# Preparing the weights of a folded CIN network: T with V2 stationary on four tiles of TensorE, turned two fields at a time, on one Trainium2 core

## The chip, the cores and the metric

The kernel runs on one core of one Trainium2 chip. The metric is the device time of one execution in microseconds, taken as the median of several runs: 757.2 us before the change (three runs, 756.5 to 758.38). The profile was taken from a run of its own, whose span from the first to the last instruction is 755.9 us. All data are fp32.

## The reference

A compressed interaction network of three layers, on a batch of 1024 samples with 39 fields of 64 elements:

```python
def _cin_layer(Xk, X0, W, b):                 # Xk (B, Hk, E), X0 (B, 39, E), W (64, Hk*39)
    Wr = W.reshape(64, Hk, 39)
    return einsum('bhe,bfe,ohf->boe', Xk, X0, Wr) + b[None, :, None]

Xk = X0
for W, b in ((W0, b0), (W1, b1), (W2, b2)):   # W0 (64, 39*39), W1 and W2 (64, 64*39)
    Xk = _cin_layer(Xk, X0, W, b)
    outs.append(Xk.sum(axis=-1))
y = concatenate(outs, -1) @ fc_w.T + fc_b     # fc_w (1, 192), y (1024, 1)
```

Only a linear function of the last two layers is wanted. So the kernel folds them: V2[o, b] is W2 contracted with the last third of fc_w, with the second third of fc_w as a 40th column, and T[h, a, b] is the sum over o of W1[o, h, a] times V2[o, b]. Then both the first layer X1[h] and its factor are quadratic forms in the fields (the factor with linear terms, for which a row of ones stands as field 40):

- X1[h] = sum over (a, b) of W0[h, a, b] x_a x_b
- Z[h] = sum over (a, b) of T[h, a, b] x_a x_b
- the result is, up to bias terms, the sum over h and the 64 elements of X1[h] times (Z[h] + fc_w[h])

## The kernel before

It has two stages. **Preparation** loads the weights, makes V2, then T and W0 with h on the partitions, in one tile `both` of 128 partitions (W0 on 0 to 63, T on 64 to 127) by 39 x 40 columns (a, b), and from that the stationary matrices: x_a x_b and x_b x_a are the same product, so their weights are added, in seven chunks of up to 128 pairs; each chunk is turned on TensorE and copied to `wa`. **The main stage** goes through 32 blocks of 2048 columns (32 samples of 64 elements); VectorE (DVE) multiplies gathered rows of fields into a tile `p` of 128 pair products, and TensorE multiplies `wa` by it.

Sizes and the tiles of the preparation:

```python
B, F, E, H = 1024, 39, 64, 64
FH = F * H
NPAIR = 6; ORDER = (0, 1, 3, 2, 4, 5); NCHUNK = NPAIR + 1
MM, SUB, BLK = 512, 1024, 2048
NA = 20; NG0 = 6; FT = F + 1
...
v2 = const.tile([H, FT], F32, name="v2")
both = const.tile([128, F * FT], F32, name="both")
...
w1s = prep.tile([H, FH], F32, name="w1s")
w0s = prep.tile([2 * F, NA * H], F32, name="w0s")
...
load(0)                                                                 # x for the first block, on SyncE's queue
nc.scalar.dma_start(fcrow, fc_w)
nc.scalar.dma_start(w2s, w2.rearrange("o (s n) -> (o s) n", s=2))
load_ones(0, nc.scalar)
nc.sync.dma_start(w1s, w1)                                              # L201
nc.scalar.dma_start(                                                    # L202
    w0s, bass.AP(w0t.tensor, w0t.offset, [[F * H, F], [(F - NA) * H, 2], [1, NA * H]])
)
```

W0 comes as (b, a, h). TensorE is kept occupied by multiplications of zeros (`spin`); V2 comes from eight matmuls on four tiles of 32 columns (L305), a transpose on DVE and copies:

```python
def spin(n):
    for _ in range(n):
        nc.tensor.matmul(idle[:, 0:128], zeros[:, 0:128], zeros[:, 0:128], start=True, stop=True)   # L224
spin(4)
...
for k in range(2):
    for u in range(4):
        f0 = u // 2 * 19 + k * 10
        nc.tensor.matmul(pv[k][32 * u : 32 * u + 32, 0:320], fc2[:, u % 2 * 32 : u % 2 * 32 + 32],  # L305
                         w2v[:, f0 : f0 + 10, :], start=True, stop=True)
...
spin(5)
for k in range(2):
    nc.vector.transpose(blocks[:, k], pv[k][:, 0:320])
```

T takes one matmul for each field a, with W1's columns of that field stationary and V2's 40 columns moving; W0 takes one transpose for two fields; both land in the four banks `pt`, which are copied to `both`:

```python
w1v = w1s.rearrange("o (h f) -> o f h", f=F)

def turn_t(g):
    for a in range(g * NG0, min((g + 1) * NG0, NA)):
        for s in range(2):
            at = (s * NG0 + a % NG0) * FT
            nc.tensor.matmul(pt[g][H:128, at : at + FT], w1v[:, a + s * (F - NA), :], v2,           # L358
                             start=True, stop=True)

turn_t(0)
for a in range(NA):
    at = a % NG0 * FT
    nc.tensor.transpose(halves_of[a // NG0][0:H, at : at + F, :],                                   # L369
                        w0s[:, a * H : a * H + H], unit[0 : 2 * F, 0 : 2 * F])
for g in range(1, 4):
    turn_t(g)
first = [prods.tile([128, BLK], F32, name="p", tag="p") for _ in range(3)]
for g in range(4):
    n = min(NG0, NA - g * NG0)
    if g % 2 == 0:
        k = g // 2
        product(0, ORDER[k], halves[0], first[k])                                                   # L165
    for s in range(2):
        ...
        (nc.vector.tensor_copy, nc.scalar.copy)[g % 2](                                             # L387
            both[:, a * FT : (a + n) * FT], pt[g][:, at : at + n * FT])
spin(4)
```

The start of the main stage. `weight_rows(c)` makes the additions of chunk c (L402 on DVE, a few plain copies on ScalarE), `weight_turn(c)` turns it (L437) and copies it to `wa` (L438), `product` makes p (L165), and `multiply` is the multiplication of the main stage (L453) for quarters of 512 columns:

```python
for c in ORDER[:3]:
    weight_rows(c)
weight_turn(0)
p = {(0, c): t for c, t in zip(ORDER, first)}
product(0, ORDER[2], halves[0], first[2])
for n, c in steps[:3]:
    product(n, c, halves[1], p[n, c])
n, c = steps[3]
weight_rows(c)
p[n, c] = product(n, c)
for k, (n, c) in enumerate(steps[:3]):
    multiply(n, c, p[n, c], (0,))
    if k < 2:
        weight_turn(steps[k + 1][1])
    multiply(n, c, p[n, c], (1,))
```

The rows that `product` multiplies come by indirect transfers (L124) into `rt`, four tiles of 128 x 2048 a block, double buffered; products are made four steps ahead of their multiplication, in four buffers.

Of the kernel before, what the change touches and what calls it, by code (L numbers as in the profile page):

```python
# [54 lines left out]
F32 = mybir.dt.float32  # L55
# [22 lines left out]
NA = 20  # L78
NG0 = 6
# [18 lines left out]
def cin_kernel(ctx: ExitStack, tc: tile.TileContext, x, w0t, b0, w1, b1, w2, b2, fc_w, fc_b, out):  # L98
# [43 lines left out]
    v2 = const.tile([H, FT], F32, name="v2")  # L142
# [28 lines left out]
    with prep as prep:  # L171
        w2s = prep.tile([128, FH // 2], F32, name="w2s")
        w1s = prep.tile([H, FH], F32, name="w1s")
        w0s = prep.tile([2 * F, NA * H], F32, name="w0s")
# [13 lines left out]

        nc.vector.memset(ones, 1.0)
        nc.vector.memset(zeros, 0.0)  # L190
        nc.vector.memset(fc2, 0.0)
        nc.vector.memset(warm, 0.0)

        def load_ones(k, engine):
# [6 lines left out]
        nc.sync.dma_start(w1s, w1)  # L201
        nc.scalar.dma_start(  # L202
            w0s, bass.AP(w0t.tensor, w0t.offset, [[F * H, F], [(F - NA) * H, 2], [1, NA * H]])
        )
# [5 lines left out]
        nc.gpsimd.memset(pairs, 0.0)  # L210
        nc.scalar.copy(warm, warm)
# [6 lines left out]
        idle = bank("idle")  # L218
        pt = [bank("pt") for _ in range(4)]


        def spin(n):
            for _ in range(n):
                nc.tensor.matmul(idle[:, 0:128], zeros[:, 0:128], zeros[:, 0:128], start=True, stop=True)  # L224

        spin(4)


# [61 lines left out]
        spin(3)  # L290
# [21 lines left out]
        for k in range(3):  # L312
            turn_row(small[0:H, k + 1 : k + 2], k)
        turn_row(small[H:128, 4:5], 0)

        for g in range(4):
            nc.tensor.matmul(
                pt[g][0:H, F : 2 * NG0 * FT : FT],
                zeros[:, 0:H],
                zeros[:, 0 : 2 * NG0],  # L320
                start=True,
                stop=True,
            )
        spin(5)
# [3 lines left out]
        nc.scalar.copy(v2[:, F:FT], small[0:H, 2:3])  # L328
        nc.vector.tensor_copy(v2[:, 0:20], column[0:H])
        nc.scalar.copy(v2[:, 20:F], column[H:128, 1:20])  # L330
# [19 lines left out]

        w1v = w1s.rearrange("o (h f) -> o f h", f=F)
        halves_of = [t[:, 0 : 2 * NG0 * FT].rearrange("p (s c) -> p c s", s=2) for t in pt]

        def turn_t(g):
            for a in range(g * NG0, min((g + 1) * NG0, NA)):
                for s in range(2):
                    at = (s * NG0 + a % NG0) * FT
                    nc.tensor.matmul(  # L358
                        pt[g][H:128, at : at + FT],
                        w1v[:, a + s * (F - NA), :],  # L360
                        v2,
                        start=True,
                        stop=True,
                    )

        turn_t(0)
        for a in range(NA):
            at = a % NG0 * FT
            nc.tensor.transpose(  # L369
                halves_of[a // NG0][0:H, at : at + F, :],  # L370
                w0s[:, a * H : a * H + H],
                unit[0 : 2 * F, 0 : 2 * F],
            )
        for g in range(1, 4):
            turn_t(g)

        first = [prods.tile([128, BLK], F32, name="p", tag="p") for _ in range(3)]
        bothv = both.rearrange("p (a b) -> p a b", b=FT)
        for g in range(4):
            n = min(NG0, NA - g * NG0)  # L380
            if g % 2 == 0:
                k = g // 2
                product(0, ORDER[k], halves[0], first[k])
            for s in range(2):
                a = g * NG0 + s * (F - NA)
                at = s * NG0 * FT
                (nc.vector.tensor_copy, nc.scalar.copy)[g % 2](  # L387
                    both[:, a * FT : (a + n) * FT], pt[g][:, at : at + n * FT]
                )
        spin(4)  # L390


    def weight_rows(c):
# [233 lines left out]
```

## Time and profile before

| what | from the profile before |
|---|---|
| time, median of three runs | 757.2 us |
| span of the profiled run | 755.9 us |
| L453, main multiplication | 1792 records, first start 27.03 us |
| L358, matmuls of T | 80 records, 11.77 to 14.84 and 17.58 to 24.45 us |
| L369, transposes of W0 | 20 records, 14.84 to 17.58 us |
| L305, V2 | 16 records, from 5.83 us, 2.56 us busy |
| L387, copies to `both` | 4 of 128x240 on DVE (400 ns each), 2 of 128x240 and 2 of 128x80 on ScalarE |
| L402, additions | 50 in all, 22 of them from 24.88 us within 2.28 us |
| share of the DMA engines, 12 to 22 us | 0.97 to 1.04 |

In the profile PE is TensorE's matmul, PEld its weight load, DVE is VectorE, ACT is ScalarE and POOL is GpSimd. A line of a group has the line of the kernel, the engine, the operation, the tiles (output, then inputs), the shapes and the count; then busy time and mean length of one; then the idle time just before it and what ended it. An fp32 matmul leaves two records, a transpose one. Records of matmuls overlap, so the number of a group times its mean is more than its busy time. The page's second part divides the span into 40 slices and gives each engine's busy share in tenths, and under PEclk the clock granted to TensorE.

### The profile page before, as it was taken

The page shows a single profiled execution, that of the slowest core. Times are in us where ns is not written, and L with a number is a line of the kernel's source. Part 1 is how long each engine was busy: PE and PEld are TensorE (multiplying, and loading weights), DVE is VectorE, ACT ScalarE, POOL GpSimd, SP SyncE. Part 2 cuts the span into 40 slices and gives each one's busy share as a digit, 9 for nine tenths or more (in the row PEclk, how much of TensorE's full clock was granted, in tenths as well). Part 3 has the DMA queues.
Part 4 walks back from the last instruction along what each step waited for, and adds up shares of the span by engine and source line. Part 5 has one row for each costly group of instructions (what it writes and reads, how often), then busy time and mean ns, then how long its engine had stood idle before and what let it go on. Part 6 is the DMA issues. An engine that isn't in the chain of part 4 may idle for free.

```text
span 755.9 us, 5394 instructions
## 1 busy us (share of the span) xinstructions
PE 749.7 (99%) x1977; PEld 335.9 (44%) x1977; DVE 641.6 (85%) x504; ACT 161.3 (21%) x218; POOL 312.9 (41%) x192
## 2 busy tenths in 40 slices
PE   8999999999999999999999999999999999999998
PEld 6644444444444444444444444444444444444443
DVE  4688988888898888898888988888889888898885
ACT  1132122111122212122221112212122221212212
POOL 5765432635324362432536333363442536343100
PEclk8699999999999999999999999999999999999999
DMA  8889577665768657577765758766576864737400
GB/s 269 338 303 362 171 319 256 244 264 186 281 205 334 243 194 293 170 279 257 285 253 179 282 183 331 255 228 272 170 271 239 317 239 164 289 138 298 167 0 0
DMA packets 58698, 180.08 MB, mean 238 GB/s; under 512 B 37050, under 2 KB 37147, under 8 KB 38512
## 3 DMA queue, kind: packets, MB, share of 16 engines
q0 software_dynamic: 24160, 169.39, 59.1%
q1 hardware_dynamic: 34225, 9.30, 5.4%
q10 hardware_dynamic: 287, 1.06, 0.5%
q8 instruction: 15, 0.25, 0.1%
q14 instruction: 11, 0.09, 0.0%
HBM read 179.67 MB, written 10.28 MB: 251 GB/s over the span
## 4 chain that ended last, share of the span: by engine, by line
PE 98%; DMA 1%; DVE 0%; SPq 0%; ACT 0%; issue 0%
PE po L453 96%; PE pt L358 1%; DMA w1s<-in_w 1%; PE pt L369 0%; PE idle L224 0%; SPq L117 0%; PE tr L437 0%; DVE g L492 0%; DVE sums L494 0%; ACT zq L491 0%; ACT wa L438 0%; DVE y L582 0%; PE py L578 0%; PE pk L500 0%; PE pk L501 0%
## 5 line engine op out<-in xcount | busy, mean ns | idle before, releaser
L453 PE MATMUL po<-p,wa 128*128 128x512 f32 (+1 forms) x1792 | 723.5, 596 | 0.4 <-ACT wa L438 0.4
L165 DVE TENSOR_TENSOR p<-r 128x2048 f32<-128x2048 f32 (+1 forms) x195 | 435.0, 2258 | 93.6 <-PE po L453 87.8
L453 PEld LDWEIGHTS po<-p,wa 128*128 128x128 f32 (+1 forms) x1792 | 313.9, 190 | 406.2 <-issue 384.8
L124 POOL DMA_INDIRECT r<-xd,lists x131 | 258.8, 1975 | 374.6 <-DVE p L165 336.7
L472 ACT ACTIVATE z<-po,fc0s 64x512 f32<-64x512 f32 x124 | 84.6, 683 | 356.6 <-PE po L453 349.8
L466 ACT COPY g<-u 39x1024 f32<-39x1024 f32 x64 | 66.6, 1043 | 180.0 <-DVE sums L483 180.0
L478 DVE SCALAR_TENSOR_TENSOR g<-po,b0s,z 64x512 f32<-64x512 f32 x124 | 86.4, 734 | 0.0
L483 DVE TENSOR_REDUCE sums<-g 103x16 f32<-103x1024 f32 x62 | 75.6, 1220 | 2.2
L167 DVE TENSOR_TENSOR p<-u,v 128x2048 f32<-128x2048 f32 x16 | 36.6, 2285 | 0.0
L124 POOL DMA_INDIRECT u<-xd,lists x16 | 28.4, 1773 | 10.2 <-DMA xd<-in_x 5.7
L124 POOL DMA_INDIRECT v<-xd,lists x16 | 16.2, 1010 | 4.9 <-issue 4.9
L358 PE MATMUL pt<-v,w1s 64*64 64x40 f32 x80 | 10.0, 311 | 1.1 <-DMA w1s<-in_w 1.1
L358 PEld LDWEIGHTS pt<-v,w1s 64*64 64x64 f32 x80 | 9.8, 212 | 1.4 <-issue 1.4
L224 PE MATMUL idle<-zeros 128*128 128x128 f32 x32 | 7.2, 394 | 1.7 <-DVE zeros L190 1.7
L492 DVE SCALAR_TENSOR_TENSOR g<-po,b0s,zq 64x512 f32<-64x512 f32 x4 | 3.0, 743 | 5.3 <-ACT zq L491 5.3
L224 PEld LDWEIGHTS idle<-zeros 128*128 128x128 f32 x32 | 6.1, 285 | 1.8 <-DVE zeros L190 1.7
L438 ACT COPY wa<-tr 128x128 f32<-128x128 f32 x7 | 1.9, 265 | 20.7 <-PE tr L437 20.7
L387 DVE COPY both<-pt 128x240 f32<-128x240 f32 x4 | 1.4, 400 | 5.7 <-PE pt L358 5.7
L402 DVE TENSOR_TENSOR pairs<-both 128x6 f32<-128x6 f32 (+27 forms) x50 | 5.3, 179 | 0.6 <-ACT both L387 0.6
L117 POOL DMA_DIRECT2D xd<-in_x x5 | 5.2, 1049 | 0.0
L491 ACT ACTIVATE zq<-po,fc0s 64x512 f32<-64x512 f32 x4 | 2.7, 683 | 10.2 <-PE po L453 10.2
L387 ACT COPY both<-pt 128x240 f32<-128x240 f32 (+1 forms) x4 | 1.0, 295 | 14.3 <-PE pt L358 14.3
(79 smaller groups left out, 39.4 us busy)
## 6 DMA issues: line engine op xcount, KB each, us to landing
xd<-in_x SPq DMA_DIRECT2D x27, 312.0 KB
r<-xd,lists POOLq DMA_INDIRECT x131, 7.6
xd<-in_x POOLq DMA_DIRECT2D x5, 312.0 KB, 7.2
w2s<-in_w ACTq DMA_DIRECT2D x1, 624.0 KB
w1s<-in_w SPq DMA_DIRECT2D x1, 624.0 KB
w0s<-in_w0t ACTq DMA_DIRECT2D x1, 390.0 KB
u<-xd,lists POOLq DMA_INDIRECT x16, 9.1
v<-xd,lists POOLq DMA_INDIRECT x16, 9.4
```

Of the source, the lines that this page charges most:

```text
L117: engine.dma_start(xd[n // 2 % NTAB][first : first + F].rearrange("f (b e) -> f b e", e=E), xv[:, n * BB : (n + 1) * BB, :],)
L124: nc.gpsimd.indirect_dma_start(dst[:, cols], None, table, bass.IndirectOffsetOnAxis(ap=lists[:, k : k + 1], axis=0), element_offset=cols.s ...
L165: nc.vector.tensor_tensor(p[:, cols], r[:, i, cols], r[:, k, cols], ALU.mult)
L167: nc.vector.tensor_tensor(p, ut[n // 2 % 2], vt[n // 2 % 2], ALU.mult)
L224: nc.tensor.matmul(idle[:, 0:128], zeros[:, 0:128], zeros[:, 0:128], start=True, stop=True)
L358: nc.tensor.matmul(pt[g][H:128, at : at + FT], w1v[:, a + s * (F - NA), :], v2, start=True, stop=True,)
L402: nc.vector.tensor_tensor(out, diagonal(a, b, sa, sb), diagonal(b, a, sb, sa), ALU.add)
L453: nc.tensor.matmul(po[n + h][m], wa[w, c, :], p[w, bass.ts(m, MM)], start=c == opens[n + h], stop=c == closes[n + h],)
L466: nc.scalar.copy(gt[H : H + F], ut[n // 2 % 2][h : h + F, bass.ts(m, SUB)])
L472: nc.scalar.activation(z[m // 2][:, bass.ts(m % 2, MM)], po[n][m][H:128], AF.Identity, bias=fc0s[H:128])
L478: nc.vector.scalar_tensor_tensor(gt[0:H, at], po[n][m][0:H], b0s, z[m // 2][:, at], ALU.add, ALU.mult)
L483: nc.vector.tensor_reduce(sums[:, b_at : b_at + SB], gt.rearrange("p (b e) -> p b e", e=E), AX.X, ALU.add)
```

## The change

T is computed the other way round: V2, padded to 64 columns and held on both halves of the partitions, is the stationary operand, and W1 moves. W1 is loaded in two halves of its h on 128 partitions, so that four matmuls of 512 columns, one on each quarter of the array, make fields 0 to 31, and two smaller ones the last seven. The result has b on the partitions. It is copied out of PSUM to SBUF (`part`, `rest`) and turned back, two fields with one transpose. W0 is turned in the same way, two fields of 64 at a time with 39 partitions in, instead of one column of two fields with 78 partitions in, and ahead of T, and goes to PSUM banks of its own. It is for a shorter sequence of instructions on TensorE between the arrival of W1 and the first multiplication. The third part concerns the first chunk: its additions, its turn and its product stand first in the queues, ahead of those of the second and third chunk; the products no longer stand among the copies. The number and place of the spins change too.

The core of the diff:

```diff
-NA = 20
-NG0 = 6
+NA = 16
+NR = F - 2 * NA
+NW = 20
...
-    v2 = const.tile([H, FT], F32, name="v2")
+    v2 = const.tile([128, H], F32, name="v2")
...
-        w1s = prep.tile([H, FH], F32, name="w1s")
-        w0s = prep.tile([2 * F, NA * H], F32, name="w0s")
+        w1s = prep.tile([128, FH // 2], F32, name="w1s")
+        w0s = prep.tile([128, NW * H], F32, name="w0s")
+        part = prep.tile([128, NA, H], F32, name="part")
+        rest = prep.tile([H, NR, H], F32, name="rest")
...
-        nc.sync.dma_start(w1s, w1)
-        nc.scalar.dma_start(
-            w0s, bass.AP(w0t.tensor, w0t.offset, [[F * H, F], [(F - NA) * H, 2], [1, NA * H]])
-        )
+        w0v = w0t.rearrange("b a h -> b (a h)")
+        nc.scalar.dma_start(w0s[0:F], w0v[:, 0 : NW * H])
+        nc.sync.dma_start(w0s[H : H + F, 0 : (F - NW) * H], w0v[:, NW * H : F * H])
+        for s, engine in enumerate((nc.sync, nc.scalar)):
+            engine.dma_start(w1s[H * s : H * s + H], w1[:, s * (FH // 2) : (s + 1) * (FH // 2)])
...
-        spin(4)
+        spin(512, pr)
...
-        spin(3)
+        spin(128, pr)
...
-        spin(5)
+
+        for k in range(NW // 2):
+            for s in range(2):
+                n = min(128, (F - NW * s) * H - k * 128)
+                nc.tensor.transpose(
+                    pw[s][0:n, k * FT : k * FT + F],
+                    w0s[H * s : H * s + F, k * 128 : k * 128 + n],
+                    unit[H * s : H * s + F, H * s : H * s + F],
+                )
...
+        copies = (nc.vector.tensor_copy, nc.scalar.copy)
+
+        def untwine(half, a, n, src, width):
+
+            for s, copy in enumerate(copies):
+                m = (n + 1 - s) // 2
+                copy(
+                    bothv[H * half : H * half + H, a + s : a + n : 2, 0:width],
+                    src[H * s : H * s + H, 0 : m * FT].rearrange("p (a b) -> p a b", b=FT)[
+                        :, :, 0:width
+                    ],
+                )
+
+        for s, (a, n) in enumerate(((0, NW), (NW, F - NW))):
+            untwine(0, a, n, pw[s], F)
...
+        for s in range(2):
+            rows = slice(H * s, H * s + H)
+            for k in range(2):
+                nc.tensor.matmul(
+                    pt[s][H * k : H * k + H],
+                    v2[rows],
+                    w1v[rows, NA * k : NA * (k + 1), :],
+                    start=True,
+                    stop=True,
+                )
+        for s in range(2):
+            rows = slice(H * s, H * s + H)
+            nc.tensor.matmul(
+                pr[rows, 0 : 32 * NR], v2[rows], w1v[rows, 2 * NA : F, :], start=True, stop=True
             )
-        for g in range(1, 4):
-            turn_t(g)
-
+        spin(128, small)
+        for s, copy in enumerate(copies):
+            at = slice(32 * s, 32 * s + 32)
+            copy(part[:, :, at], pt[s].rearrange("b (a h) -> b a h", h=32))
+        for s, copy in enumerate(copies):
+            at = slice(32 * s, 32 * s + 32)
+            copy(
+                rest[:, :, at],
+                pr[H * s : H * s + H, 0 : 32 * NR].rearrange("b (a h) -> b a h", h=32),
+            )
+        for k in range(3):
+            src = part if k < 2 else rest
+            rows = slice(H * (k % 2), H * (k % 2) + FT)
+            n = NA if k < 2 else NR
+            to = (pv[0], pv[1], pr)[k]
+            for a in range(0, n, 2):
+                m = min(2, n - a)
+                nc.tensor.transpose(
+                    to[0 : m * H, a // 2 * FT : a // 2 * FT + FT],
+                    src[rows, a : a + m, :].rearrange("b a h -> b (a h)"),
+                    unit[rows, rows],
+                )
+            untwine(1, NA * k, n, to, FT)
+        for _ in range(2):
+            spin(256, small)
...
-    for c in ORDER[:3]:
+    p = {}
+    for k, (n, c) in enumerate(steps[:3]):
+        p[n, c] = first[k]
         weight_rows(c)
-    weight_turn(0)
-    p = {(0, c): t for c, t in zip(ORDER, first)}
-    product(0, ORDER[2], halves[0], first[2])
+        if not k:
+            weight_turn(c)
+            spin(256, small)
+        product(n, c, halves[0], p[n, c])
     for n, c in steps[:3]:
         product(n, c, halves[1], p[n, c])
```

In the new form `spin(n, to)` is one multiplication of zeros with n moving columns.

## The prediction

> **What bounds the kernel now.** I read the page from the top: shares of the engines, slices, chain, then groups by line.
>
> ```profile
> PE 749.7 (99%) x1977; PEld 335.9 (44%) x1977; DVE 641.6 (85%) x504; ACT 161.3 (21%) x218; POOL 312.9 (41%) x192
> ...
> PE   8999999999999999999999999999999999999998
> PEclk8699999999999999999999999999999999999999
> ...
> L453 PE MATMUL po<-p,wa 128*128 128x512 f32 (+1 forms) x1792 | 723.5, 596 | 0.4 <-ACT wa L438 0.4
> L358 PE MATMUL pt<-v,w1s 64*64 64x40 f32 x80 | 10.0, 311 | 1.1 <-DMA w1s<-in_w 1.1
> ```
>
> TensorE is busy for 749.7 of 755.9 us, and 723.5 us of that is line 453, the main multiplication, which the change leaves alone. DVE's largest idle time is spent waiting for L453 (87.8 us of L165's 93.6). So the long stage is TensorE's, and the only thing that can move is the moment at which L453 starts. The second slice of PEclk reads 6: something in the first 40 us runs at a reduced clock. The chain of work that ended last shows the preparation in order:
>
> ```profile
> 1.82 9.81 DMA w1s<-in_w
> 11.63 0.14 issue
> 11.77 3.07 PE pt L358 x24
> 14.84 2.74 PE pt L369 x20
> 17.58 6.87 PE pt L358 x56
> 24.45 2.00 PE idle L224 x8
> 26.46 0.23 PE tr L437
> 26.68 0.02 issue
> 26.71 0.27 ACT wa L438
> 26.98 0.04 issue
> 27.03 2.07 PE po L453 x2
> ```
>
> The columns are start, length, what. Nothing before 11.77 us can be helped by cheaper arithmetic: it is W1 arriving. From 11.77 to 24.45 TensorE turns W1 into T (L358, 80 records) and turns W0 (L369, 20), back to back. Then come 2.6 us of spins, additions, turn and copy until 27.03. The change attacks those last 15.3 us.
>
> The table of stages gives the clock: 1.00 to 12 us, 0.93 in 12 to 14, 0.50 from 14 to 30, 0.80 in 30 to 32, then 1.00. The first value is not to be trusted. The 128x128 spins last 421 ns each around 3 us and 275 ns around 10 us, so the clock was already half at first and went up near 9.5 us. So the preparation runs slow almost throughout, and so does the beginning of the main stage (27.03 to about 30.8).
>
> [...] the 16 records of L305, on four tiles of 32 columns, lie within 2.56 us though each lasts 771 ns; they start in fours, 0.6 us apart. [...] The DMA share here is about 1.0 from 4 to 22 us[...]. [...]
>
> **The change, part by part.**
>
> *Landing of W1.* The bytes stay: W1 624 KB, and W0 39 x 39 x 64 x 4 B = 380 KB where 390 KB went before (one field was loaded twice). But both halves of W1 now stand behind W0 in their queues. Before, T could begin at 11.77. I take 12.2, by 0.4 us of later issue (the W0 issue takes 0.96 us on its queue, part of it hidden).
>
> *W0's transposes* (20, as before, now 39x128 in and two fields at a time) move ahead of T into the wait for W1. L369 costs 2.81/20 = 0.14 us each, so 2.8 us go off the path, if W0 lands by about 9.5. L305 ended at 8.4, so there is room. The copies of W0 out of PSUM (about 390 elements, twice on each of DVE and ACT) fit there as well.
>
> *T.* 80 records of 64x40, 9.94 us (3.07 + 6.87, 124 ns each) go. In their place: four matmuls with V2 stationary and 512 moving columns, one on each 64x64 tile, and two of 224 columns. At half clock a pass of 320 columns takes 0.6 us (L305), so one of 512 takes 0.96, and two passes on four tiles side by side 1.9 us, with 0.2 us to drain (771 minus 600 ns): 2.1 us. T is complete at 14.3. The two small ones run on beside the copies.
>
> *New: T has to be copied and turned.* Copies of 128x512 out of PSUM: DVE has 398 ns for 240 elements[...]; ACT's z of 64x512 takes 0.683. They run in parallel, 0.8 us with the handover: 15.1. Then 20 transposes of 40x128 at L369's 0.14 us: 2.8 us, 17.9. Their copies into both follow group by group; only the last (four columns of transposes, 160 elements for DVE) is on the path, 0.3 plus 0.1: 18.3.
>
> *First chunk.* 22 additions of L402 took 2.28 us, 0.1 each; chunk 0 has six: 0.6 us, 18.9. Before, all three chunks' rows stood in the queue of DVE but the products of the first two had been made earlier, in DVE's idle time from 14.84. Now the product follows the rows: 1.22 us, ready at 20.1. On TensorE: two spins of 256 columns from 17.9, 0.86 us each at half clock (the chain's later piece of 16 records of L453, 8 multiplications of 512 columns, takes 6.87 us at full clock, 0.86 each; half the columns at half the clock is the same), end at 19.6; the turn (0.42) and ACT's copy (0.27) give 20.4; one more spin of 0.85 stands behind the turn, to about 20.9. So L453 starts at about 20.8.
>
> The sum: 27.03 - 20.8 = 6.2 us earlier. As a cross-check, 12.7 us of T and W0 become 2.1 + 0.8 + 2.8 + 0.4 = 6.1 (saves 6.6), W1 costs 0.4, and the end part goes from 2.58 to 2.5.
>
> *Afterwards* L453 must stay fed. At half clock TensorE takes 1.7 us for a quarter and DVE (rows 0.6 plus 1.22) keeps up. At full clock it would wait some 0.4 us for the third chunk's product (10 additions, 1.0 + 1.22). I deduct 0.3 us. Transfers: bytes moved per us, summed from 24 us on at 1.05 MB a gather, put the second block's tiles in place by about 34, 36, 38.5 and 41 us; their products began at 44.27, 46.90 and later and would now begin some 6 us sooner, still after them. The gain should arrive in full at the end: 757.2 - 6.2 + 0.3 = 751.3.
>
> **Rivals.**
>
> *TensorE's clock decides.* [...] Before, 3.8 us of L453 ran at half clock, a loss of 1.9 us. [...]
>
> *W0 or W1 late.* If W0 lands with W1, the transposes of W0 stand ahead of T in TensorE's order and go back on the path: 2.8 us, 754. For it: the DMA engines are full. Against: W0 is now ahead of W1 in both queues.
>
> *Tiles do not overlap.* If row and column tiles together ran one by one, T would take 4 x 1.9 + 1.7 us: some 6 us lost, 757. The four column tiles of L305[...] speak against it.
>
> *The transfers or DVE become the bound after the start,* so that an earlier start only makes TensorE wait. DVE is 85% busy, and the gathers at 1.0 share until 44 us speak for it; the slack counted above (2 us at the tightest, plus products made ahead) against it. The gain would shrink to 3 or 4 us.
>
> **Range and chances.** From these: 751.3 us, with 748.5 to 754.5 holding it 8 times in 10; the width is W1's landing (0.7 either way), the clock (2) and W0 (2.8 with a small chance). 2% is 15.1 us, and the whole preparation that the change can touch is 15.3 us, so "faster by over 2%" would need it to vanish: 0.01. For slower by 2% I see no mechanism: 0.01.
>
> **What would show it.** In the changed profile: six T matmuls (12 records) within about 3 us from about 12; W0's transposes before them, with no idle time on TensorE for W0 after W1 is there; the 20 transposes of T within 2.5 to 3.5 us; L453's first start near 20.8 rather than 27.03; L453's total near 723 and its idle time under 1 us. The prediction is wrong if W1 is waited for beyond 13.5 us, if T's records start one after another, if the transposes cost over 0.2 us each, or if L453 shows waits for p or for gathers after its start.

## The result and the profile after

| | before | after |
|---|---|---|
| time, median | 756.85 us (four runs, 756.24 to 758.38) | 751.37 us (four runs, 750.06 to 751.82) |
| ratio, 95% interval | | 0.9922 (0.9902 to 0.9942) |
| span of the profiled run | 755.9 us | 748.3 us |
| main multiplication (L453, now L482), first start | 27.03 us | 21.12 us |
| the same, busy in all | 723.5 us | 721.9 us |
| half clock after that start | 3.76 us | 0.52 us |

The predicted 751.3 us was met. The profiled run was the fastest of its four (750.06 us); part of that is the clock, as is shown further down. Lines of the page of the kernel after: the engines' shares, two rows of the 40 slices, and two groups (busy time and mean of one in ns, then idle time before them).

```profile
PE 739.5 (99%) x1903; PEld 322.7 (43%) x1903; DVE 643.5 (86%) x509; ACT 163.8 (22%) x223; POOL 319.3 (43%) x193
...
PE   7999999999999999999999999999999999999998
...
PEclk8999999999999999999999999999999999999999
...
L482 PE MATMUL po<-p,wa 128*128 128x512 f32 (+1 forms) x1792 | 721.9, 595 | 0.0
...
L382 PE MATMUL pt<-w1s,v 64*64 64x512 f32 x8 | 2.2, 1107 | 1.4 <-DMA w1s<-in_w 1.4
```

L482 has the same 1792 records and no idle time before any of them, although DVE is at 86%. So nothing took the gain back after the start; the 6 in the second slice of PEclk is gone as well. T is now 8 records in 2.2 us, and 4 small ones of 224 columns behind them, instead of 80 in 10.0. The first slice of PE reads 7: TensorE is idle more of the time during the preparation, and the preparation is shorter.

The chain of work that ended last, of the kernel after (start, length, what):

```profile
2.62 7.63 DMA w1s<-in_w
10.25 0.75 issue
11.00 2.18 PE pt L382 x8
13.18 0.82 PE pr L391 x4
14.00 0.72 PE small L232 x2
14.72 0.59 issue
15.31 2.27 PE pv L411 x16
17.58 0.02 issue
17.60 0.49 DVE both L369
...
18.84 0.26 ACT both L369
...
19.27 0.58 DVE pairs L431 x5
...
21.29 1.19 PE po L482 x2
```

It has the order that the prediction gave it: W1, T, copies, transposes, copies, additions, start. Three lengths look odd. `pv L411` stands in the chain for 2.27 us although, as the timeline below shows, its records lie within 0.96 us; and 0.59 us of "issue", for which the profile names no reason, stand before it. These two turned out to be the same thing, and its cause is the one thing here that stayed open. Then 0.75 us of "issue" stand between the landing of W1 at 10.25 us and T, where the chain of the kernel before had 0.14; the 10.25 is not to be trusted, as comes out below.

### The profile page after: what moved, and what is told of

Same layout as the page of the kernel before. It is cut to its first block, busy times and chain, and to the rows that moved or that the text cites. A ratio compares the mean times of both kernels' runs of the same rounds, so it can differ in the third digit from the quotient of the medians.

```text
span 748.3 us, 5266 instructions
## 1 busy us (share of the span) xinstructions
PE 739.5 (99%) x1903; PEld 322.7 (43%) x1903; DVE 643.5 (86%) x509; ACT 163.8 (22%) x223; POOL 319.3 (43%) x193
## 4 chain that ended last, share of the span: by engine, by line
PE 97%; DMA 1%; DVE 0%; issue 0%; SPq 0%; ACT 0%
PE po L482 96%; DMA w1s<-in_w 1%; PE pv L411 0%; PE pt L382 0%; PE small L232 0%; PE tr L466 0%; SPq L118 0%; ACT both L369 0%; PE pr L391 0%; SPq L208 0%; DVE g L521 0%; DVE sums L523 0%; ACT zq L520 0%; DVE pairs L431 0%; DVE both L369 0%
## 5 line engine op out<-in xcount | busy, mean ns | idle before, releaser
L482 PE MATMUL po<-p,wa 128*128 128x512 f32 (+1 forms) x1792 | 721.9, 595 | 0.0
L482 PEld LDWEIGHTS po<-p,wa 128*128 128x128 f32 (+1 forms) x1792 | 313.5, 190 | 405.0 <-issue 383.5
L125 POOL DMA_INDIRECT u<-xd,lists x16 | 33.0, 2062 | 9.8 <-DMA xd<-in_x 5.2
L125 POOL DMA_INDIRECT v<-xd,lists x16 | 20.3, 1269 | 4.9 <-issue 4.9
L232 PE MATMUL pr<-zeros 128*128 128x512 f32 (+1 forms) x4 | 2.9, 822 | 1.7 <-DVE zeros L194 1.7
L232 PE MATMUL small<-zeros 128*128 128x256 f32 (+1 forms) x8 | 3.7, 591 | 0.0
L382 PE MATMUL pt<-w1s,v 64*64 64x512 f32 x8 | 2.2, 1107 | 1.4 <-DMA w1s<-in_w 1.4
L523 DVE TENSOR_REDUCE sums<-g 103x8 f32<-103x512 f32 x4 | 2.7, 686 | 0.1
L610 PE MATMUL py<-sums,wfin 103*1 103x512 f32 (+2 forms) x6 | 2.1, 448 | 0.6 <-DVE sums L523 0.6
```

The costliest lines, as they stand in the source:

```text
L125: nc.gpsimd.indirect_dma_start(dst[:, cols], None, table, bass.IndirectOffsetOnAxis(ap=lists[:, k : k + 1], axis=0), element_offset=cols.s ...
L232: nc.tensor.matmul(to[:, 0:n], zeros[:, 0:128], zeros[:, 0:n], start=True, stop=True)
L482: nc.tensor.matmul(po[n + h][m], wa[w, c, :], p[w, bass.ts(m, MM)], start=c == opens[n + h], stop=c == closes[n + h],)
```

## The experiments

Eleven runs followed, in three groups; within a group all ran on one chip, beside the kernel before. The first group ran on one chip, the second and the third on another, both on the same; the chip of the result above is not on record. The kernel before took 756.74, 756.74 and 757.29 us in the three groups. The table has all of them, with the moment at which the main multiplication starts, and how long the clock is still half after it. The latter can be read from the table of stages to within some 0.02 us: the clock is 1.00 or 0.50 between its changes, so in a stretch of 2 us with a mean clock s, 4 x (1 - s) us were at half clock.

| kernel | group | time, us (range) | ratio to before (95%) | span | start | half clock after it | span - start - half of the half-clock time |
|---|---|---|---|---|---|---|---|
| before | | 756.85 | | 755.9 | 27.03 | 3.76 | 727.0 |
| after | | 751.37 (750.06 to 751.82) | 0.9922 (0.9902 to 0.9942) | 748.3 | 21.12 | 0.52 | 726.9 |
| same: after, again | 1 | 747.83 (746.87 to 748.43) | 0.9884 (0.9867 to 0.9900) | 745.7 | 18.63 | 0 | 727.1 |
| w0_rows | 1 | 749.06 (748.57 to 749.83) | 0.9901 (0.9884 to 0.9918) | 747.3 | 20.25 | 0 | 727.1 |
| t_rows | 1 | 751.46 (751.22 to 753.09) | 0.9937 (0.9921 to 0.9954) | 749.8 | 22.25 | 1.20 | 727.0 |
| old_order | 1 | 751.66 (751.31 to 752.55) | 0.9938 (0.9921 to 0.9954) | 749.6 | 20.81 | 3.85 | 726.9 |
| same2: after, again | 2 | 751.75 (751.51 to 751.93) | 0.9935 (0.9911 to 0.9959) | 750.2 | 21.07 | 4.39 | 726.9 |
| no_spins | 2 | 750.98 (750.60 to 751.94) | 0.9924 (0.9900 to 0.9949) | 750.1 | 20.49 | 5.53 | 726.8 |
| warm | 2 | 751.78 (751.47 to 751.92) | 0.9937 (0.9913 to 0.9961) | 749.7 | 21.00 | 3.56 | 726.9 |
| all | 2 | 750.59 (750.25 to 751.75) | 0.9925 (0.9899 to 0.9950) | 748.7 | 20.84 | 1.90 | 726.9 |
| same3: after, again | 3 | 751.36 (750.31 to 752.81) | 0.9928 (0.9911 to 0.9946) | 748.5 | 21.29 | 0.64 | 726.9 |
| late_gathers | 3 | 751.58 (one run) | | 749.8 | 20.75 | 4.28 | 726.9 |
| rows_both | 3 | 753.38 (one run) | | 751.6 | 23.51 | 2.40 | 726.9 |

The last column is the reason why so little has to be explained after the start: in thirteen profiles the span is the start, plus half of the half-clock time that follows, plus 726.8 to 727.1 us. Whatever the change did, it did through these two numbers.

The numbers come from lines like these, out of the tables of stages (stretch, its length, then busy time and records of PE, PEld, DVE, ACT and POOL, then the clock, the DMA share and GB/s). Of after:

```profile
20.00:22.00 2.00, 2.00 (x5) 1.18 (x6) 2.00 (x8) 0.49 (x3) 0.00 (x0) 0.59 1.04 422
```

and of same2:

```profile
24.00:26.00 2.00, 2.00 (x4) 0.79 (x3) 2.00 (x3) 0.00 (x0) 2.00 (x1) 0.64 0.06 25
```

In after, 4 x 0.41 = 1.64 us at half clock from 20 on, so full speed at 21.64; in same2, 4 x 0.36 = 1.44 us, so full speed only at about 25.4. The two starts differ by 0.05 us and the spans by 1.9 us: it is the clock. The four runs of same3 lie at 750.31, 750.33, 752.38 and 752.81 us, which fits two such outcomes (their mean clocks are 0.995 twice and 0.993 twice), but the table has a start for only one of them.

### The kernel after, again (same)

No edit.

> The changed kernel once more, unaltered, for a second profile. If the time that the change brings is the earlier start of the main multiplication alone (5.9 us in the first profile, from 27.03 to 21.12 us), its first start lies again within 0.5 us of 21.1 and only the granted clock around it moves the end. [...] Time 750 to 752 us.

747.83 us, where 750 to 752 was expected, and 3.5 us less than the first time, with the kernel before at its usual 756.74. Lines of the timeline of same (start, length, engine, line, what; in brackets the idle time before it and what ended it):

```profile
8.67 0.79 PE L328 MATMUL pw<-unit,w0s 39*128 39x39 f32 x20 [0.39 <-DMA w0s<-in_w0t]
10.53 2.18 PE L382 MATMUL pt<-w1s,v 64*64 64x512 f32 x8 [1.07 <-DMA w1s<-in_w]
10.54 1.02 DVE L369 COPY both<-pw 64x390 f32<-64x390 f32 x2
12.62 0.69 DVE L397 COPY part<-pt 128x512 f32<-128x512 f32 x1 [1.06 <-PE pt L382]
13.57 0.38 DVE L400 COPY rest<-pr 64x224 f32<-64x224 f32 x1 [0.25 <-PE pr L391]
14.18 0.97 PE L411 MATMUL pv<-unit,part 40*128 40x40 f32 x13
15.11 0.88 DVE L369 COPY both<-pv 64x320 f32<-64x320 f32 x2 [1.16 <-PE pv L411]
15.63 0.82 ACT L369 COPY both<-pv 64x320 f32<-64x320 f32 x2 [1.30 <-DVE both L369]
16.63 0.71 DVE L431 TENSOR_TENSOR pairs<-both 128x36 f32<-128x36 f32 x6 [0.41 <-ACT both L369]
18.63 1.10 PE L482 MATMUL po<-p,wa 128*128 128x512 f32 x2 [0.40 <-DVE p L166]
```

And of after, the same kernel in its first profile:

```profile
11.77 1.03 DVE L369 COPY both<-pw 64x390 f32<-64x390 f32 x2 [1.09 <-remote]
...
13.92 0.69 DVE L397 COPY part<-pt 128x512 f32<-128x512 f32 x1 [1.13 <-PE pt L382]
...
15.31 0.96 PE L411 MATMUL pv<-unit,part 40*128 40x40 f32 x16 [0.59 <-issue]
16.79 0.38 DVE L400 COPY rest<-pr 64x224 f32<-64x224 f32 x1 [2.18 <-PE pv L411]
...
19.13 0.71 DVE L431 TENSOR_TENSOR pairs<-both 128x36 f32<-128x36 f32 x6 [0.41 <-ACT both L369]
```

In same each copy follows its matmuls at once: T's first 512-column matmuls end at 12.59 and DVE copies at 12.62; `pr` ends at 13.53 and is copied at 13.57. In after, W0's transposes end at 9.62 by their records and are copied at 11.77, T's at 13.05 and 13.92, `pr` at 14.00 and 16.79. DVE was idle for 1.1 to 2.2 us before each. So the results of TensorE were released 0.9 to 2.8 us later than its records, whose ends are modelled, say. Stage by stage the two starts differ by 0.47 us (W1 there at 11.00, not 10.53), 0.66 (T's last record to the first transpose: 2.13 against 1.47), 1.37 (first transpose to the first addition: 3.82 against 2.45) and -0.01 (from there to the start); the sum is the whole 2.49.

### W0 on one set of partitions (w0_rows)

```diff
-        w0s = prep.tile([128, NW * H], F32, name="w0s")
+        w0s = prep.tile([F, F * H], F32, name="w0s")
...
-        nc.sync.dma_start(w0s[H : H + F, 0 : (F - NW) * H], w0v[:, NW * H : F * H])
+        nc.sync.dma_start(w0s[:, NW * H : F * H], w0v[:, NW * H : F * H])
...
-                    w0s[H * s : H * s + F, k * 128 : k * 128 + n],
-                    unit[H * s : H * s + F, H * s : H * s + F],
+                    w0s[:, s * NW * H + k * 128 : s * NW * H + k * 128 + n],
+                    unit[0:F, 0:F],
```

> W0's two parts side by side on partitions 0 to 38, so that all 20 transposes of W0 use one row group; in the changed kernel they alternate between rows 0 and 64, their records start 31 ns apart and end at 9.6 us, but the copies out of them begin at 11.77. Theory A (the records are right, and the release of the copies lags because two row groups are in use): the copies of W0 begin by 10.8 us, when DVE is free, and the first main multiplication moves by under 0.3 us since W0 is not on the path. Theory B (the records' starts are issue times, and the array really takes about 0.145 us for each transpose): records 0.12 to 0.15 us apart up to about 11.6 us, the copies at 11.7 as before, and T not earlier. Under both the time is 750 to 752.5 us.

The same bytes, from the same two queues, but both parts on partitions 0 to 38. Of w0_rows, from the timeline:

```profile
9.98 1.38 PE L328 MATMUL pw<-unit,w0s 39*128 39x39 f32 x20 [1.71 <-DVE fields_of L349]
...
11.90 2.18 PE L382 MATMUL pt<-w1s,v 64*64 64x512 f32 x8 [0.55 <-DMA w1s<-in_w]
```

W0's transposes start at 9.98 instead of 8.67 us and take 1.38 us instead of 0.79; W1, behind it in the queues, is waited for until 11.90 instead of 10.53. The start is 1.62 us later and the time 1.23 us longer. W0 beside itself on two sets of partitions is worth that; the transposes themselves end at 11.36 and stand just before W1, which is still the last to come. The expectation had W0 off the path under both of its theories, and 750 to 752.5 us: it had not seen that W1 comes later with W0. Its question, why the copies lag, gets no answer here, for in this group same, with its two sets of rows, has no lag either.

### W1 on 64 partitions, T on two tiles (t_rows)

```diff
-        w1s = prep.tile([128, FH // 2], F32, name="w1s")
+        w1s = prep.tile([H, FH], F32, name="w1s")
...
-            engine.dma_start(w1s[H * s : H * s + H], w1[:, s * (FH // 2) : (s + 1) * (FH // 2)])
+            at = slice(s * (FH // 2), (s + 1) * (FH // 2))
+            engine.dma_start(w1s[:, at], w1[:, at])
...
-                    v2[rows],
-                    w1v[rows, NA * k : NA * (k + 1), :],
+                    v2[0:H],
+                    w1v[:, NA * k : NA * (k + 1), 32 * s : 32 * s + 32],
...
```

> W1 whole on 64 partitions, still in two transfers, so that T's matmuls use rows 0 to 63 and only two column tiles instead of four tiles. If four tiles run side by side, T's matmuls take twice as long here, about 3.7 us for four of them at half clock against 1.9, and the small two 1.5 against 0.8: T complete 2 to 2.5 us later, the main multiplication from about 23 us, time 752.5 to 754. If the four tiles run in pairs only, nothing is lost: start at 21.1, 751 to 752. If the lag of the copies behind the records (0.9 to 2.8 us in the changed kernel) comes from the two row groups, it goes, and gives back some of the loss: start at about 21.5 to 22.

Both halves of W1 keep their size and their queue and only change their place. Of t_rows, from the timeline:

```profile
12.17 3.92 PE L383 MATMUL pt<-w1s,v 64*64 64x512 f32 x8 [1.89 <-ACT both L370]
```

T starts at 12.17 us, 1.64 us later, and its eight records take 3.92 us instead of 2.18: with one set of rows only two tiles work side by side. (The releaser named is ACT's copy, which ended at 12.03; but in same T ran beside that copy. W1's last landing signal in the trace of t_rows is at 12.03 too, and that is what T waits for.) The first stage is seen in the table of stages, of same:

```profile
8.00:10.00 2.00, 1.06 (x24) 0.70 (x20) 1.48 (x10) 0.76 (x4) 1.70 (x2) 1.00 0.83 251
```

and of t_rows:

```profile
8.00:10.00 2.00, 1.00 (x21) 0.74 (x18) 1.49 (x10) 0.75 (x4) 1.70 (x2) 1.00 0.92 187
```

The DMA engines are busier (0.92 against 0.83) and move less (187 against 251 GB/s). The higher share went with the lower rate. The two effects, 1.64 and 1.74 us, are 3.38 of the 3.62 us by which the start is later; the time is 3.63 us longer. The doubling of T was expected; the later W1 was in none of the expectation's theories, which had T complete 2 to 2.5 us later at most.

### The additions and products in the old order (old_order)

```diff
+            if k != 1:
+                product(0, ORDER[k // 2], halves[0], first[k // 2])
             untwine(1, NA * k, n, to, FT)
...
-    for k, (n, c) in enumerate(steps[:3]):
-        p[n, c] = first[k]
-        weight_rows(c)
-        if not k:
-            weight_turn(c)
-            spin(256, small)
-        product(n, c, halves[0], p[n, c])
+    for c in ORDER[:3]:
+        weight_rows(c)
+    weight_turn(0)
+    p = {(0, c): t for c, t in zip(ORDER, first)}
+    product(0, ORDER[2], halves[0], first[2])
```

> The third part of the change undone: the products of the first two chunks stand among the copies again, the additions of three chunks stand ahead, the last spin goes. By the prediction's account the product of 1.22 us is then off the path but the copies behind it are 1.2 us later each: both products are ahead of the last copies, so the additions begin 1.2 to 2.4 us later than 19.13, the turn follows 0.8 later, and the main multiplication starts at 22.2 to 23.4 us: 752 to 753.5 us. If DVE's idle time before the copies (2.2 us in the changed kernel, before the copy of the last seven fields) can take the products, the loss is under 0.5 us.

This undoes the third part of the change alone (one spin goes with it). From its timeline:

```profile
15.09 1.23 DVE L166 TENSOR_TENSOR p<-r 128x1024 f32<-128x1024 f32 x1 [1.23 <-DMA r<-xd,lists]
...
19.15 2.25 DVE L433 TENSOR_TENSOR pairs<-both 128x36 f32<-128x36 f32 x22 [0.32 <-ACT both L369]
...
20.81 2.07 PE L484 MATMUL po<-p,wa 128*128 128x512 f32 x2 [0.35 <-ACT wa L469]
```

The product of 15.09, and a second one at 17.26, stand in DVE's queue among the copies of T, and the additions begin at 19.15 instead of 16.63. The start is 2.18 us later. Besides, TensorE has nothing to do from 16.24 to 20.01 us, and the clock is half until 24.66, 3.85 us into the main stage, which costs 1.93 us more (that the one brings the other is not shown). The two make 4.1 us; the spans differ by 3.9 and the times by 3.83 us. So the third part, a few lines that only move instructions, is worth 3.8 of the 8.9 us by which the change shortens the time in this group: about 2.2 by the start, and the rest by the clock, which differs by more than that between profiles of one kernel (no half clock after the start in same, 4.39 us in same2).

### The spins: none, or one more (no_spins, warm)

The kernel after ran again beside them as same2.

> The changed kernel a third time. In its first profile the copies behind TensorE began 0.9 to 2.8 us after the modelled end of the matmuls they wait for, and the main multiplication at 21.12 us; in the second they began at once, and it started at 18.63. Theory A (the lag belongs to the chip or the session of the first profile): no lag again, start at 18.4 to 19.2 us, time 746.5 to 749. Theory B (the lag comes and goes from execution to execution): the four times spread over 747 to 752, and the profile may show either. Theory C (the second profile was the odd one): start near 21.1, time 750 to 752.

It showed the late releases of the first profile again: copies of W0 at 12.08, of `rest` at 16.40, start at 21.07 us. Without any spin:

```diff
         def spin(n, to):
-            nc.tensor.matmul(to[:, 0:n], zeros[:, 0:128], zeros[:, 0:n], start=True, stop=True)
+            pass
```

> All seven multiplications of zeros left out. If the spins of 256 columns and the one behind the first turn stood on the path, the main multiplication starts up to 0.3 us earlier; in the second profile it was DVE's product that came last, so the start should stay within 0.2 us of 18.6. Theory of the clock: [...] time 749.5 to 751.5. Rival: [...] the spins are ballast: time within 0.7 us of the changed kernel on the same chip.

750.98 us against 751.75, with ranges that overlap. The profile has the start 0.58 us earlier, and the half clock 5.53 us into the main stage instead of 4.39, which is 0.57 us: what is won in the queue is lost in the clock. With a spin of 512 columns between W0's transposes and T:

```diff
                     unit[H * s : H * s + F, H * s : H * s + F],
                 )
+        spin(512, pr)
```

> One more spin of 512 columns (0.86 us at full clock, 1.7 at half) in TensorE's idle time between W0's transposes and the arrival of W1. In the second profile the clock fell to half at 11.29 us and T's eight records took 2.18 us. Theory of the clock: [...] T's eight records take 1.1 to 1.3 us, the main multiplication starts 0.8 to 1.2 us earlier (17.5 to 17.9 us), time 0.8 to 1.5 us less than the changed kernel on the same chip. Rival: the spin runs at half clock or W1 lands earlier than it ends, and T begins up to 0.7 us later: start 18.6 to 19.3 us, no gain.

751.78 us: no gain. The clock was full until 17.73 us (1.00 in each stretch from 8 to 16 us, 0.93 from 16 to 18). But of warm:

```profile
9.91 1.13 PE L232 MATMUL pr<-zeros 128*128 128x512 f32 x2
...
11.07 2.18 PE L383 MATMUL pt<-w1s,v 64*64 64x512 f32 x8
```

The spin takes 1.13 us where one of the same shape takes 2.1 at the beginning (in same); T's records take 2.18 us, exactly as in same, where the clock was half for all but the first 0.8 us of them. T did not become faster with the clock. The late releases stayed too (W0 copied at 11.97, `rest` at 15.61). And at 17.73, 3.3 us ahead of the start, the clock fell to half.

### More work taken out at once (all)

The spin of warm, the products of the first three chunks in the order of their use with the first in quarters, and the copies to `both` split by group, so that ScalarE need not wait for DVE. The first multiplications are regrouped to go with that.

```diff
-            for s, copy in enumerate(copies):
+            for s, copy in enumerate(copies if n < NA else (copies[a // NA],) * 2):
...
-        product(n, c, halves[0], p[n, c])
-    for n, c in steps[:3]:
+            product(n, c, slice(0, MM), p[n, c])
+            product(n, c, slice(MM, SUB), p[n, c])
+        else:
+            product(n, c, halves[0], p[n, c])
         product(n, c, halves[1], p[n, c])
...
```

> The spin of the run before, and two more steps: the first chunks' products in the order of their use (each chunk's rows and both halves of its product before the next chunk, the first half in two quarters), and the copies of T into the common tile divided between DVE and ScalarE by group, not by every other field, so that neither waits for the other. In the second profile ScalarE's copies all began behind DVE's and ended at 16.6 us against 16.2, and the first multiplication waited for a product of 1.23 us. Expected: copies done 0.2 to 0.3 us earlier, the first quarter's product ready after 0.68 instead of 1.22 us, so that the turn and its copy decide: start 0.6 us earlier than the run before (17.0 to 17.4 us), and TensorE without a wait for products after it. Time 1.0 to 2.2 us less than the changed kernel on the same chip. If DVE becomes the bound in the first 15 us of the main stage, TensorE waits there for p, visible as idle time before L482-like records of up to 1 us, and the gain stays at that of the spin.

750.59 us, 1.2 less than same2 beside it and 0.8 less than same3 in the next group, whose range (750.31 to 752.81) covers it. In the profiles the start is only 0.23 us earlier than in same2 (20.84), and the half clock after it 2.49 us shorter, 1.25 us in time. So the time lies in the expected range, but not in the expected way, for the start was to come 0.6 us earlier than in warm and came 0.16 earlier. The gain is chiefly the same swing of the clock that runs of one and the same kernel show. It isn't shown to be a better kernel, and no version here clearly beats the changed one.

### Where the late release comes from (same3, late_gathers, rows_both)

In the third group the kernel after ran once more, beside two edits that each were to take away one suspect.

> The changed kernel again, as the reference of this call's chip. So far it started its main multiplication at 21.12, 18.63 and 21.07 us in three profiles; in the two late ones the copies of W0 and of T's last fields were released 1.5 to 2.8 us after the modelled end of their transposes and matmuls, in the early one at once. Expected: one of the two patterns, 747 to 748.5 us with the early one, 751 to 752 with the late one.

Late again, at 21.29 us. From the timeline of same3:

```profile
9.04 0.79 PE L328 MATMUL pw<-unit,w0s 39*128 39x39 f32 x20 [0.76 <-DMA w0s<-in_w0t]
...
13.35 1.03 DVE L369 COPY both<-pw 64x390 f32<-64x390 f32 x2 [2.71 <-PE pt L382]
...
16.95 0.38 DVE L400 COPY rest<-pr 64x224 f32<-64x224 f32 x1 [1.48 <-remote]
```

W0's transposes end by their records at 9.83 and are released 3.5 us later; `pr`, at 14.04, 2.9 us later. The first suspect: the gathers, which GpSimd issues from 7.62 us on in this kernel. late_gathers moves the making of their lists (two small DVE operations), and with it all gathers, behind DVE's copies of W0:

```diff
-        nc.vector.tensor_copy(lists[:, 0:4], fields_of[:, 0:4])
-        nc.vector.tensor_scalar(lists[:, 4:8], fields_of[:, 0:4], float(FT), None, ALU.add)
...
-        for cols in halves:
-            roll(0, (0, 1, 2), cols)
...
             untwine(0, a, n, pw[s], F)
+        nc.vector.tensor_copy(lists[:, 0:4], fields_of[:, 0:4])
+        nc.vector.tensor_scalar(lists[:, 4:8], fields_of[:, 0:4], float(FT), None, ALU.add)
+        for cols in halves:
+            roll(0, (0, 1, 2), cols)
...
```

> The indices of the gathers are written only after the copies of W0, so that no gather is in flight before; the first product then waits for its gathers, and the main multiplication starts later by design, at 21 to 24 us. What is asked is the release of W0's copies. Theory A (TensorE's completions are held up while the first gathers are on their way: on the late chip the copies began at 11.95 to 12.08 us in four kernels whose transposes ended at 9.99 to 10.60, just as the first gather landed): on a chip with the late pattern the copies now begin within 0.15 us of the end of the transposes, or as soon as DVE is free at 10.4. Theory B (it has nothing to do with the gathers): they still begin at about 12.0 us. On a chip with the early pattern nothing is decided.

```profile
10.53 1.02 DVE L355 COPY both<-pw 64x390 f32<-64x390 f32 x2
...
11.92 1.17 POOL L125 DMA_INDIRECT r<-xd,lists  x1 [8.82 <-DVE lists L365]
...
14.09 0.38 DVE L400 COPY rest<-pr 64x224 f32<-64x224 f32 x1 [0.25 <-PE pr L391]
...
17.58 0.72 DVE L431 TENSOR_TENSOR pairs<-both 128x36 f32<-128x36 f32 x6 [0.32 <-issue]
...
19.37 1.23 DVE L166 TENSOR_TENSOR p<-r 128x1024 f32<-128x1024 f32 x1 [1.08 <-DMA r<-xd,lists]
```

Up to here the lateness is gone: W0's records end at 10.11, DVE copies them at 10.53 as soon as it is free, and `rest` follows `pr` (14.06) at once. Behind that some of it is back: the records of T's transposes end at 15.70 and the additions begin 1.88 us later, in same 1.29. The additions begin at 17.58 instead of 19.30. But the first product now has to wait for its gather (19.37, the last line), and the start is 20.75: what the early release gives is lost to the later gathers, and the half clock lasts 4.28 us after it. So this is no better kernel. It also doesn't settle the cause. With the gathers the edit took away what they move: the share of the DMA engines is 0.03 from 10 to 12 us and 0.09 from 12 to 14, in same3 1.06 and 0.84, and when `pr` was released two gathers had been issued and had hardly begun to move data. Such traffic can't be the cause alone, for in same the share is 0.83 to 0.97 from 10 to 16 us and nothing is late. The second suspect: transposes and matmuls that alternate between the two sets of rows of the array. rows_both is w0_rows and t_rows together, so that everything in the preparation but T's own transposes uses rows 0 to 63.

> W0 and W1 both on the first partitions alone (39 and 64), so that all transposes of W0 and all of T's matmuls use one row group. Theory A (the late release comes from alternating between two row groups): on a chip with the late pattern W0's copies are released within 0.15 us of the last transpose, and those of T's last fields too. Theory B: they are released late as in the changed kernel. In any case W1 lands later than on 128 partitions, at 11.5 to 12.5 us, and T takes 3.9 us for its first four matmuls; start of the main multiplication at 22 to 23.5 us.

```profile
10.84 1.39 PE L329 MATMUL pw<-unit,w0s 39*128 39x39 f32 x20 [2.56 <-DMA w0s<-in_w0t]
12.23 1.11 DVE L370 COPY both<-pw 64x390 f32<-64x390 f32 x2 [1.64 <-PE pw L329]
...
18.21 0.38 DVE L401 COPY rest<-pr 64x224 f32<-64x224 f32 x1 [1.99 <-PE pr L392]
```

Here the lateness is gone throughout, with the gathers at their old place (first issue 7.83 us): W0 at 12.23 as its records end, `rest` at 18.21 after `pr` at 18.17. It costs about what w0_rows and t_rows cost together (a start 4.88 us later than in same, where they had 1.62 and 3.62): 23.51. Either edit removed the lateness, late_gathers in its first part only and each in one profile; and in the first group the unedited kernel didn't have it at all, nor did w0_rows, t_rows and old_order there. In rows_both W0's transposes also come much later (10.84 us, against 9.04 to 9.81 in the profiles of groups 2 and 3 that had the lateness), so that there the moment itself could matter.

Two more things separate the groups. One is the chip: no profile from the chip of the first group is late, and all late ones whose chip is known are from the other; but the two edits ran on that other chip too, one with no lateness and one with little. No run tells the chip from the rest. The other is in the traces. Of the updates of semaphores, the signals that end the waits, 175 to 186 are recorded from 8 to 18 us in the four profiles of the first group, and only 66 to 78 in after and in the five late ones of groups 2 and 3. So in the late profiles a named releaser ("remote", "issue", or `pv` for the copy of `rest`) is not to be trusted, nor is the landing of W1 at 10.25 us in after: of its half from SyncE's queue the trace has three signals there and 16 in same. In late_gathers, which has these signals, W1's last one is at 10.92 us. The starts of the instructions don't depend on such records. Whether the lost records and the late release have one cause wasn't tried; rows_both has only 75 records as well, and prompt copies.

The cause stays open. What is measured is its size: about 2.5 us of start and, with the clock, 3.5 to 3.9 us of time between one group and the others.

## Why the prediction was right, and where its steps were not

**The mechanism** is as predicted. The gain is an earlier start, 27.03 to 21.12 us, and the main stage is untouched. The rival that transfers or DVE become the bound is refuted: L482 has no idle time in after, and the last column of the table has the same 727 us for all. The deduction of 0.3 us for waits was not needed.

**The start** was put at 20.8 and came at 21.12. But that is a sum of errors that cancel, and so the number was met by luck (its last step even ends at 20.9, not 20.8, by its own spins):

| stage | predicted | same | after |
|---|---|---|---|
| T begins (W1 there) | 12.2 | 10.53 | 11.00 |
| T's 512-column matmuls | 2.1 | 2.18 | 2.18 |
| their end to the first transpose of T | 0.8 | 1.47 | 2.13 |
| to the first addition | 3.2 | 2.45 | 3.82 |
| to the first L482 | 2.5 | 2.00 | 1.99 |
| start | 20.8 | 18.63 | 21.12 |

*W1's landing* is the step that was wrong in kind: it counted the bytes and the place in the queues, and nothing else. The place where they land counts too. With W1 on 64 partitions, as in the kernel before, T began at 12.17 us (t_rows), close to the predicted 12.2 and 1.64 us later than with W1 on 128; with W0 on one set of 39 partitions its transposes began at 9.98 us, 1.31 us later than with W0 on two (w0_rows), each with the same bytes and queues. Why the place counts wasn't tried apart.

*T on four tiles* is right in size: 2.18 us for the predicted 2.1, and on two tiles 3.92, so that the rival "tiles do not overlap" is refuted. From two 64x64 tiles to four that is a factor of 1.8. The argument by half clock did not hold: T takes 2.18 us at full clock too (warm).

*The copies of T* were taken as parallel, 0.8 us with the handover. Those of `part` do run side by side (0.69 us from 12.62 on DVE and 0.58 us from 12.75 on ScalarE in same), and they end 0.62 us after T's matmuls; but in TensorE's own queue the small matmuls (to 13.53) and a spin (0.72 us) still stand before the first transpose: 1.47 us. Without spins it was 0.76 (no_spins: 13.61 to 14.37). *The last copies* to `both` were put at 0.4 us; they are 1.3 in same, from the last transpose at 15.34 to the first addition at 16.63, because ScalarE's copy waits for DVE's (15.63, "1.30 <-DVE both"): their columns interleave in one tile, and they go one after the other. The copies of W0 speak for the interleaving as the reason: divided by group they begin together (12.00 and 12.04 us in all), by every other field 0.59 us apart (12.08 and 12.67 in same2).

*The transposes* were mis-sized the other way: 0.14 us each, taken from the old ones of 78 partitions, and so 2.8 us for 20. All 20 lie within 14.18 to 15.34 in same, 1.2 us, and W0's 20 within 0.79 us, off the path as predicted. Part of the difference is the clock: the old 20 ran at half clock, and where the new 20 of T do so from first to last they take 1.53 us (w0_rows, 15.56 to 17.09, with single records of 0.30 us), while they take 0.99 in late_gathers (14.71 to 15.70, with single records of 0.23 us), almost all at full clock.

*The late release* was in no step. It put back in after what W1 and the transposes had won. Where it is absent (group 1), the same kernel takes 747.83 us, below the low end of the range.

**The clock.** This rival was half right. In the first profile the half clock ended 0.52 us after the start instead of 3.76, a gain of 1.6 us that brings the profiled run to 750.06; in same2 it ended 4.39 us after, a loss. (The prediction read from the spins that the clock of the kernel before had gone up near 9.5 us; the granted clock in the trace is full from 6.89 and half from 13.72.) What moves the clock was not shown. In after it changes at 11.40, 14.82, 18.23 and 21.64 us, in steps of 3.41. Where the changes lie differs from one profile to the next of the same kernel (the first fall to half is at 11.29 us in same, 11.40 in after and 11.80 in same2), and so does the clock that the start meets. Neither removing the spins nor adding one changed the time clearly (750.98 and 751.78 us beside 751.75).

**The third part** was priced as keeping the end part the same (2.5 for 2.58 us). By itself it is worth 2.18 us of start (old_order): the prediction had counted the old order's products as standing in DVE's idle time, and with the shorter T there is none left to hide them.

## What to carry to other kernels

Price an instruction sequence in front of a long stage by its chain alone, and then check the stage after the start with one subtraction (span less start less half of the half-clock time): here it showed at once that nothing else had changed. When a load is waited for, look at the partitions on which it lands as well as its bytes and its queue (here T began 1.64 us later with W1 on 64 partitions instead of 128); a high share in the DMA column doesn't say that the rate is high (0.92 came with 187 GB/s, 0.83 with 251). When a stage gets shorter, look again at what used to be hidden in it: the products in DVE's queue, in its idle time before, cost 2.2 us of start here when they were put back, and 3.8 us of time with the clock.

## What the runs showed that was not expected

- The same kernel took 747.83 us in one group and 751.75 and 751.36 in two others, while the kernel before took 756.74, 756.74 and 757.29 beside it. The start differs by 2.4 to 2.7 us, most of it in the release of TensorE's results between 9 and 17 us, up to 3.5 us after the modelled end of their records; the rest of the time is the clock. The cause is open.
- 64x64 matmuls of 512 columns on four tiles took 2.18 us for eight records both in after, where the clock was half for all but the first 0.4 us of them, and in warm, at full clock throughout, whereas the first two records of the main multiplication (128x128, 512 columns) took 2.05 us at half clock (warm, from 21.00) and 1.10 at full clock (same, from 18.63).
- Transposes of 39 or 40 partitions by 128 columns followed one another within 31 to 62 ns: W0's 20 took 0.79 us alternating between two sets of rows (same, clock 1.00 from 8 to 10 us) and 1.38 us on one (w0_rows), with a median record of 229 ns in both.
- With W1 going to 64 partitions the DMA engines moved 187 GB/s at a share of 0.92, and with W1 going to 128 partitions 251 GB/s at a share of 0.83, both from 8 to 10 us.
